# Eight more gather buffers and eight more sample buffers in the first four stages of a deformable-convolution and mixture-of-experts kernel

## The chip, the cores and the metric

The kernel runs on one core of one Trainium2 chip. The metric is device time in microseconds: 7486.86 us is the median of three runs before the change. Engines are named as in the profile: PE is TensorE (PEld its weight loads), ACT is ScalarE, DVE is VectorE, POOL is GpSimd, SP is SyncE. They run at once and wait for each other through semaphores; each works through its own instructions in order.

## The reference, cut to what matters

An image batch of 4 x 256 channels x 64 x 64 goes through three deformable 3x3 convolutions and then, as tokens, through a mixture of eight experts with the two best of each token.

```python
x0 = ln_c(x)                                   # normalised over channels
for w_off, b_off, w, b in three_layers:
    om   = conv3x3(x0, w_off) + b_off          # 27 channels: 9 x (dy, dx), 9 masks
    ys, xs = grid + taps + om[:, :18]          # 9 sampling points of each pixel
    smp  = bilinear(x0, ys, xs) * sigmoid(om[:, 18:])    # [B, 256, 9, H, W]
    x0   = relu(einsum("bikhw,oik->bohw", smp, w) + b)
x = x + x0
t = tokens(x)                                  # 16384 x 256
p = softmax(ln(t) @ gate_w + gate_b); keep the best two of eight
t = t + sum over the two of p_e * (gelu(ln(t) @ W1_e + b1_e) @ W2_e + b2_e)
```

## The kernel before, in words

The convolutions run as twelve stages, one for each layer `l` and image `b`, in the order that `run` lists: (0,0), (1,0), (0,1), (2,0), (1,1), (0,2), (2,1), (1,2), (0,3), (2,2), (1,3), (2,3). Stage 3, layer 2 of image 0, is thus the one that finishes the first image. A stage has eight blocks `n` of 512 pixels; a block has nine taps `k`; a tap has four tiles of 128 pixels. So a stage is 72 taps and 288 samples.

For each sample, `samples` does four things. POOL issues an indirect DMA that gathers, for 128 pixels, a row of 1024 numbers (the four neighbours of the sampling point, L503) from a table in DRAM into a tile `g`. VectorE blends the neighbours in two instructions (L509 in place in `g`, L514 from `g` into a tile `s`). ScalarE scales `s` by mask and corner weight, in place (L517). The tiles `g` come from a ring of `GB = 10` buffers (`gat`), the tiles `s` from a ring of 8 (`smp`). A gather waits until VectorE has read the buffer's last tenant, and L514 waits until TensorE has read the last tenant of its `s`.

`turn` lags two pairs of samples behind (`LAG`): TensorE transposes a pair (L532) into PSUM and ScalarE copies it into `sT` (L535). When both pairs of a tap are there, `finish` multiplies the tap before it with its weights into `acc` (L555). After the ninth tap ScalarE takes `acc` to the next layer's window (L577), or, in layer 2, to `tokens`. In a stage's last block `finish` also loads the next stage's weights tap by tap on SP (`wk`, L477).

Side work is spread between the taps by `step` and `pump`, as generators that go on by a piece. `off_block` makes the plan of a later block: the offset convolution (L357), `om` (L366), `pm` (L371), `pos` (L391, on VectorE from L395) and so on to indices and weights. `pre_block` normalises an image that comes later: a load `xc`, transposes (L442), `h_pre` (L447, normalised at L62 to L78), stores into its table (L338) and transposes into the window (L462). In stages 0, 3 and 6 the next images' `pre_block`s run beside. `tokens`, beside stages of layer 2 and the head of the stage after them, loads the input again (`xr_tok`, L596), adds (L599), transposes (`t_tok`, L613), computes logits and normalises (`st_tok` L62, `lg_tok`, `sm_tok` L665) and stores (L626, L636). Where a generator must not go ahead of the samples, its instructions are placed on the engine after the newest sample, with `with self.after(self.last)`.

The experts start once an image's tokens are routed, from stage 4 on. They use three pools: `ffn` (their activations, and `ta`, the token rows that the results are added to, L902), `rt` (routing) and `gyp` (gathered results).

All pools are opened at the start and stay open to the end. A scheduler in the language layer places the instructions on each engine's queue from the program's order and the tiles' dependences, and puts in the semaphore waits. Indirect DMAs on POOL carry eight semaphores in turn, and a gather also waits for the one eight before it.

Of the kernel before, what the change touches and what calls it, by code (L numbers as in the profile page):

```python
# [8 lines left out]
F32 = mybir.dt.float32  # L9
# [5 lines left out]
P = 128  # L15
H = W = 64
C = 256
CC = C // P
K = 9
NL = 3  # L20
# [15 lines left out]
FT = 1 << FT_LOG  # L36
FU = FT // P
GB = 10
LAG = 2
LEAST = 2.0**-30  # L40
WINN = CC * (RPB + 2) * W
# [41 lines left out]
class Group:  # L83


    def __init__(self, b, n0, n1):
        self.b, self.n0, self.n1 = b, n0, n1
        self.nm = f"{b}_{n0}"
        self.M = (n1 - n0) * TPB

        self.NF = 2 * self.M * P // FT + E - 1


        self.half = (self.NF + 1) // 2
        self.zt, self.acc, self.gy, self.sums, self.py = {}, [], [], [], None
        self.order = [s // 2 + s % 2 * self.half for s in range(self.NF)]
# [21 lines left out]
class Weave:  # L118
# [3 lines left out]
    def __init__(self, ctx, tc, ins, out):  # L122
        nc = self.nc = tc.nc
        self.tc = tc
        self.ins = ins
        self.x = ins["x"].rearrange("b (c p) h w -> b p c (h w)", p=P)
        self.out_v = out.rearrange("b (c p) h w -> b p c (h w)", p=P)
        self.B = self.x.shape[0]

        def pool(name, bufs, **kw):  # L130
            return ctx.enter_context(tc.tile_pool(name=name, bufs=bufs, **kw))

        self.cst = pool("cst", 1)
        self.dram = pool("dram", 1, space=bass.MemoryType.DRAM)
        self.wkp = pool("wkp", 1)
        self.plan = pool("plan", 19)
        self.win = pool("win", 3)
        self.wt = pool("wt", 2)
        self.small = pool("small", 1)
        self.big = pool("big", 2)  # L140
        self.ffn = pool("ffn", 2)
        self.rt = pool("rt", 1)
        self.rt2 = pool("rt2", 2)
        self.gyp = pool("gyp", 4)
        self.smT = pool("smT", 2)
        self.smp = pool("smp", 8)
        self.gat = pool("gat", GB)
        self.ps = pool("ps", 3, space=bass.MemoryType.PSUM)
        self.ps1 = pool("ps1", 1, space=bass.MemoryType.PSUM)

        self.routes, self.tiles, self.sums = Lane(), Lane(), Lane()
        self.side, self.plans_side = [], []
        self.last = self.gathered = self.turned = None
        self.starting, self.draining, self.later = True, False, []
        self.pend, self.pairs = None, []
# [319 lines left out]
    def load_tap(self, l, k, i):  # L475
# [3 lines left out]
        )  # L479
        self.wk[k] = wk  # L480

    def main_block(self, i, n, wins):
        l, b = self.stages[i]
        plan = self.plans.pop((l, b, n))
        for k in range(K):
            for t0 in range(0, TPB, 2):
                ss = self.samples(i, n, k, t0, plan)
                self.pairs.append((i, n, k, t0, wins, ss))
                if len(self.pairs) > LAG:
                    self.turn()  # L490
            self.step(k)
            self.pump()

    def samples(self, i, n, k, t0, plan):


        nc = self.nc
        idx, cf = plan
        ss = []
        for t in (t0, t0 + 1):  # L500
            j = t * K + k
            g = self.gat.tile([P, 2, 2, C], F32, tag="g", name=f"g_{i}_{n}_{j}")
            self.gathered = nc.gpsimd.indirect_dma_start(  # L503
                out=g.rearrange("p x s f -> p (x s f)"),
                out_offset=None,
                in_=self.table(*self.stages[i]),
                in_offset=bass.IndirectOffsetOnAxis(ap=idx[:, j : j + 1], axis=0),
            )
            nc.vector.scalar_tensor_tensor(  # L509
                g[:, :, 0, :], g[:, :, 1, :], cf[:, j, 0:1], g[:, :, 0, :],  # L510
                ALU.mult, ALU.add,
            )
            s = self.smp.tile([P, C], F32, tag="s", name=f"s_{i}_{n}_{j}")
            self.last = nc.vector.scalar_tensor_tensor(  # L514
                s, g[:, 1, 0, :], cf[:, j, 1:2], g[:, 0, 0, :], ALU.mult, ALU.add
            )
            nc.scalar.activation(s, s, AF.Copy, scale=cf[:, j, 2:3])  # L517
            ss.append(s)
        return ss
# [515 lines left out]
    def run(self):  # L1035

        self.stages = [
            (0, 0), (1, 0), (0, 1), (2, 0), (1, 1), (0, 2),
            (2, 1), (1, 2), (0, 3), (2, 2), (1, 3), (2, 3),
        ]  # L1040

        beside = {0: 1, 3: 2, 6: 3}


        last = self.B - 1
        self.groups = [Group(b, 0, NB) for b in range(last)]
        self.groups += [Group(last, 0, NB // 2), Group(last, NB // 2, NB)]

        for i, (g, pace) in enumerate(zip(self.groups, (5.0, 5.0, 2.0, 1.5, 0.0))):
            g.i, g.pace, g.last = i, pace, i + 1 == len(self.groups)  # L1050
        self.plans = {}
        wins = {}
        pre = [self.pre_block(0, n, wins, n // 2 % 2 == 0) for n in range(NB)]
        for gen in pre[:3]:
            next(gen)
        self.constants()
        self.tables_init()
        for n, gen in enumerate(pre):
            for _ in gen:
                pass  # L1060

            for later in pre[n + 1 : n + 2]:
                for _ in range(3):
                    next(later)
            for later in pre[n + 3 : n + 4]:
                next(later)
            self.settle()
        self.starting = False
        for k in range(K):
            self.load_tap(0, k, 0)  # L1070
        self.ffn_constants()
        for i, (l, b) in enumerate(self.stages):
            wins, pre = {}, {}
            for n in range(NB):
                for gen in self.later[:2]:
                    self.aside(6, gen, True)
                self.later = self.later[2:]
                self.main_block(i, n, wins)
                if i in beside:
                    self.aside(5, self.pre_block(beside[i], n, pre, i == 0))  # L1080
            if i + 1 == len(self.stages) or self.stages[i + 1] == (l + 1, b):
                while self.pairs:
                    self.turn()
                self.finish()
                self.settle()
        while self.routes.pieces or self.tiles.pieces or self.sums.pieces:
            self.drain(3)
# [48 lines left out]
```

## Time and profile before

| | |
|---|---|
| median of three runs | 7486.86 us (7480.8 to 7520.67) |
| the profiled execution | 7520.62 us, its span 7518.9 us |
| busy, share of the span | PE 86%, PEld 48%, DVE 66%, ACT 43%, POOL 60% |
| granted TensorE clock | 0.944 |
| DMA engines | 2223.73 MB, mean 296 GB/s; 73.3% of their time in POOL's indirect DMAs |
| gathers | 3456 of 128 rows of 4 KB each |

Windows that fall on the gathers of the first stages (us from the start of the span): stage 0 93 to 652, stage 1 652 to 1118, stage 2 1118 to 1597, stage 3 1597 to 2095. A window's row gives the busy time of each engine, with the number of instructions in brackets. In a row of waits, "A <- B: total, times, longest" means that engine and line A sat idle until B ended; "issue" is idle time for which no releaser is seen, and "remote" a releaser that the profile doesn't name. The groups of instructions give count, busy time, mean duration and, after the second bar, idle time before them with what ended it.

### The profile page before, as it was taken

To read this page: it belongs to the slowest core of one execution; us is meant where nothing else is said; L and a number is where in the kernel's file an instruction comes from. 1 tells how busy PE (TensorE), PEld (TensorE's weight loads), DVE (VectorE), ACT (ScalarE), POOL (GpSimd) and SP (SyncE) were. 2 spreads that over 40 slices of the span, in tenths; PEclk is the share of its full clock that TensorE was granted. 3 is DMA by queue.
4 is the path that set the end of the run, shared out by engine and by line. 5 is a ranking of instruction groups with operands and counts; after the bars stand their busy time and mean duration, and the time that the engine had idled before them with its cause. 6 is when DMAs were issued, how large, how long until landed. Compare 5 with 4: busy or idle time off the path is not lost.

```text
span 7518.9 us, 88985 instructions
## 1 busy us (share of the span) xinstructions
PE 6443.2 (86%) x26500; PEld 3618.8 (48%) x26500; DVE 4952.9 (66%) x11467; ACT 3266.0 (43%) x7141; POOL 4476.5 (60%) x4245
## 2 busy tenths in 40 slices
PE   6898888888898888889988888888888788977887
PEld 3443333334454444445554445444544555644565
DVE  6776777768887666567777556666768554667421
ACT  3444544445544444445443434444444333444322
POOL 4654666656666565556557656555656565666543
PEclk8999999999999999999999999999999899989998
DMA  8997999989998888888888888888888777888644
GB/s 266 337 325 274 352 342 335 346 331 356 362 349 311 300 305 297 278 315 322 314 293 316 293 280 314 295 302 294 308 306 299 251 271 240 288 302 287 211 139 123
DMA packets 800320, 2223.73 MB, mean 296 GB/s; under 512 B 104729, under 2 KB 302873, under 8 KB 794081
## 3 DMA queue, kind: packets, MB, share of 16 engines
q0 software_dynamic: 551200, 1947.35, 73.3%
q1 hardware_dynamic: 248640, 270.69, 10.9%
q8 instruction: 215, 3.52, 0.2%
q14 instruction: 265, 2.16, 0.1%
HBM read 2160.68 MB, written 196.40 MB: 313 GB/s over the span
## 4 chain that ended last, share of the span: by engine, by line
PE 69%; ACT 10%; issue 7%; another core or an unknown queue 6%; DVE 4%; DMA 2%; POOL 1%; SPq 0%; ACTq 0%; DVEq 0%; POOLq 0%
PE acc L555 34%; PE tp L532 10%; PE ph L856 7%; PE py L874 6%; PE po L357 6%; ACT sT L535 4%; ACT s L517 3%; DVE g L509 2%; DVE s L514 1%; PE pm L371 1%; ACT hT L866 1%; PE ftp L840 1%; ACT win L577 1%; PE tpv L325 1%
## 5 line engine op out<-in xcount | busy, mean ns | idle before, releaser
L503 POOL DMA_INDIRECT g<-tab,idx x3456 | 3685.4, 1066 | 2371.6 <-DVE s L514 1061.8
L555 PE MATMUL acc<-sT,wk 128*128 128x512 f32 x6912 | 3492.1, 620 | 253.4 <-ACT sT L535 147.5
L509 DVE SCALAR_TENSOR_TENSOR g<-g,cf 128x512 f32<-128x512 f32 x3456 | 2559.2, 742 | 269.1 <-DMA g<-tab,idx 245.5
L514 DVE SCALAR_TENSOR_TENSOR s<-g,cf 128x256 f32<-128x256 f32 x3456 | 1662.7, 483 | 1331.3 <-PE tp L532 729.9
L535 ACT COPY sT<-tp 128x512 f32<-128x512 f32 x1728 | 1002.0, 585 | 2312.0 <-PE tp L532 1553.0
L517 ACT ACTIVATE s<-s,cf 128x256 f32<-128x256 f32 x3456 | 1629.5, 508 | 256.7 <-DVE s L514 160.7
L555 PEld LDWEIGHTS acc<-sT,wk 128*128 128x128 f32 x6912 | 1198.9, 198 | 1106.7 <-issue 816.7
L532 PEld LDWEIGHTS tp<-ident,s 128*128 128x128 f32 x6912 | 893.2, 146 | 1666.2 <-issue 898.9
L532 PE MATMUL tp<-ident,s 128*128 128x128 f32 x6912 | 1287.3, 286 | 439.2 <-ACT s L517 253.8
L856 PE MATMUL ph<-fzT,w 128*128 128x256 f32 x2608 | 720.8, 411 | 78.0 <-ACT fzT L844 28.1
L874 PE MATMUL py<-w,hT 128*128 128x256 f32 x2608 | 671.1, 396 | 103.5 <-ACT hT L866 58.0
L856 PEld LDWEIGHTS ph<-fzT,w 128*128 128x128 f32 x2608 | 506.3, 205 | 212.9 <-issue 69.6
L874 PEld LDWEIGHTS py<-w,hT 128*128 128x128 f32 x2608 | 484.5, 196 | 242.0 <-issue 91.9
L866 ACT ACTIVATE hT<-ph,w 128x256 f32<-128x256 f32 x652 | 281.9, 471 | 616.3 <-PE ph L856 378.2
L812 POOL DMA_INDIRECT zt<-z,tok x326 | 333.8, 1024 | 161.5 <-issue 88.0
L800 POOL DMA_INDIRECT w<-in_W,wrow x163 | 178.0, 1092 | 381.2 <-issue 138.8
L357 PE MATMUL po<-win,wo 128*32 128x504 f32 (+1 forms) x2304 | 366.0, 615 | 6.5 <-ACT win L301 4.2
L892 DVE TENSOR_TENSOR y<-py,w 128x512 f32<-128x512 f32 x163 | 111.9, 686 | 341.5 <-PE py L874 285.1
L915 POOL DMA_INDIRECT gy<-ys,slots x256 | 255.6, 998 | 104.5 <-issue 70.0
L930 DVE SCALAR_TENSOR_TENSOR ta<-gy,cw,ta 128x256 f32<-128x256 f32 x256 | 120.6, 480 | 125.6 <-DMA gy<-ys,slots 78.4
L357 PE MATMUL po<-win_pre,wo 128*32 128x504 f32 (+1 forms) x1152 | 184.2, 617 | 2.0 <-ACT om L366 2.0
L366 ACT ACTIVATE om<-po,bo 128x512 f32<-128x512 f32 x96 | 65.9, 687 | 265.3 <-PE po L357 156.3
(154 smaller groups left out, 2961.0 us busy)
## 6 DMA issues: line engine op xcount, KB each, us to landing
tab<-hv SPq DMA_DIRECT2D x512, 128.0 KB
g<-tab,idx POOLq DMA_INDIRECT x3456
ys<-y SPq DMA_DIRECT2D x163, 256.0 KB
tab<-h_pre SPq DMA_DIRECT2D x128, 256.0 KB
wk<-in_conv_w SPq DMA_DIRECT2D x99, 256.0 KB
xc_pre<-in_x SPq DMA_DIRECT2D x32, 512.0 KB
xr_tok<-in_x SPq DMA_DIRECT2D x32, 512.0 KB
t<-t_tok SPq DMA_DIRECT2D x32, 512.0 KB
```

The lines of the kernel that those rows point to most:

```text
L357: nc.tensor.matmul(po[g * Q : (g + 1) * Q, :].rearrange("q (r w) -> q r w", w=W)[:, :, x0:x1], lhsT=self.wo[l][:, 3 * ky + kx, c, :], rhs= ...
L503: self.gathered = nc.gpsimd.indirect_dma_start(out=g.rearrange("p x s f -> p (x s f)"), out_offset=None, in_=self.table(*self.stages[i]), ...
L509: nc.vector.scalar_tensor_tensor(g[:, :, 0, :], g[:, :, 1, :], cf[:, j, 0:1], g[:, :, 0, :], ALU.mult, ALU.add,)
L514: self.last = nc.vector.scalar_tensor_tensor(s, g[:, 1, 0, :], cf[:, j, 1:2], g[:, 0, 0, :], ALU.mult, ALU.add)
L517: nc.scalar.activation(s, s, AF.Copy, scale=cf[:, j, 2:3])
L532: self.turned = nc.tensor.transpose(tp[:, c, u * P : (u + 1) * P], ss[u][:, c * P : (c + 1) * P], self.ident)
L535: nc.scalar.copy(self.sT[:, :, t0 * P : (t0 + 2) * P], tp)
L555: nc.tensor.matmul(acc[:, o, :], lhsT=self.wk[k][:, c, o * P : (o + 1) * P], rhs=sT[:, c, :], start=(k == 0 and c == 0), stop=(k == K - 1 ...
L812: self.nc.gpsimd.indirect_dma_start(out=zt, out_offset=None, in_=grp.zd, in_offset=bass.IndirectOffsetOnAxis(ap=grp.tok[:, j : j + 1], axi ...
L856: nc.tensor.matmul(ph[:, h, :], lhsT=w1[:, o : o + P], rhs=zT[:, c, :], start=(c == 0), stop=(c == CC - 1),)
L866: nc.scalar.activation(ht[:, h, :], ph[:, h, :], AF.Gelu, bias=w1[:, k : k + 1])
L874: nc.tensor.matmul(py[:, u, :], lhsT=hT[h // 2][:, h % 2, u * P : (u + 1) * P], rhs=w2[:, h * C : (h + 1) * C], start=(h == 0), stop=(h == ...
```

## The change

The pools `ffn`, `rt` and `gyp` are no longer opened at the start. Two pools of eight buffers, `gatx` and `smpx`, are opened in an `ExitStack` of their own, `early`. A counter `drawn` takes the tile `g` from `gat` ten times and from `gatx` eight times in turn, and `s` from `smp` eight times and from `smpx` eight times: rings of 18 and 16. When the stage after (2, 0) begins, which is stage 4, `late_pools` closes `early`, sets the rings back to `gat` (10) and `smp` (8), and opens `ffn`, `rt` and `gyp` on the room that came free. The tiles of the last samples of stage 3 that TensorE has yet to transpose are kept by the dependences that the language layer records.

```diff
+GS = 8
+GX = 8
@@ __init__
-        self.ffn = pool("ffn", 2)
-        self.rt = pool("rt", 1)
         self.rt2 = pool("rt2", 2)
-        self.gyp = pool("gyp", 4)
         self.smT = pool("smT", 2)
-        self.smp = pool("smp", 8)
+        self.smp = pool("smp", GS)
         self.gat = pool("gat", GB)
+        self.pool = pool
+        self.early = ctx.enter_context(ExitStack())
+        more = [
+            self.early.enter_context(tc.tile_pool(name=name, bufs=GX))
+            for name in ("gatx", "smpx")
+        ]
+        self.gats = [self.gat] * GB + [more[0]] * GX
+        self.smps = [self.smp] * GS + [more[1]] * GX
+        self.drawn = 0
@@
+    def late_pools(self):
+
+        self.early.close()
+        self.gats, self.smps = [self.gat], [self.smp]
+        self.ffn = self.pool("ffn", 2)
+        self.rt = self.pool("rt", 1)
+        self.gyp = self.pool("gyp", 4)
@@ samples
-            g = self.gat.tile([P, 2, 2, C], F32, tag="g", name=f"g_{i}_{n}_{j}")
+            g = self.gats[self.drawn % len(self.gats)].tile(
+                [P, 2, 2, C], F32, tag="g", name=f"g_{i}_{n}_{j}"
+            )
@@
-            s = self.smp.tile([P, C], F32, tag="s", name=f"s_{i}_{n}_{j}")
+            s = self.smps[self.drawn % len(self.smps)].tile(
+                [P, C], F32, tag="s", name=f"s_{i}_{n}_{j}"
+            )
+            self.drawn += 1
@@ run
             wins, pre = {}, {}
+            if self.stages[i - 1] == (NL - 1, 0):
+                self.late_pools()
             for n in range(NB):
```

## The prediction

> **What bounds the kernel now.** The page comes first. Its costliest idle time, read by size, makes the change look large.
>
> ```profile
> L503 POOL DMA_INDIRECT g<-tab,idx x3456 | 3685.4, 1066 | 2371.6 <-DVE s L514 1061.8
> L514 DVE SCALAR_TENSOR_TENSOR s<-g,cf 128x256 f32<-128x256 f32 x3456 | 1662.7, 483 | 1331.3 <-PE tp L532 729.9
> ```
>
> POOL sits idle before gathers until VectorE has written a sample (a gather buffer comes free), and VectorE sits idle before samples until TensorE has transposed one (a sample buffer comes free). Both are waits for buffers, and the change doubles these buffers in stages 0 to 3. But a wait for a buffer is back pressure: it says that the waiting engine is ahead. What counts is what the engine behind all of them, TensorE, waits for. The windows of the four stages concerned, second column on: length, then busy time of PE, PEld, DVE, ACT, POOL, then clock, DMA share, GB/s:
>
> ```profile
> 93.00:652.00 559.00, 488.29 (x2064) 221.20 (x2058) 406.38 (x1015) 254.21 (x575) 310.22 (x289) 0.96 0.88 312
> 652.00:1118.00 466.00, 387.99 (x1465) 175.49 (x1466) 340.40 (x675) 214.90 (x475) 306.10 (x288) 0.96 0.93 340
> 1118.00:1597.00 479.00, 411.64 (x1564) 186.62 (x1563) 347.47 (x689) 226.38 (x501) 307.18 (x288) 0.97 0.92 339
> 1597.00:2095.00 498.00, 435.22 (x1791) 225.31 (x1792) 421.44 (x1101) 250.60 (x548) 315.71 (x288) 0.95 0.96 356
> ```
>
> TensorE is busy 83 to 87% in each. In stages 1 and 2 VectorE is busy 73%; in stage 3, which adds the image-2 normalisation and the token work, 85%. The chain of waits in the middle of stage 1 (start, length, what) shows one whole tap:
>
> ```profile
> 1000.10 0.85 PE tp L532 x4
> 1000.97 0.59 ACT sT L535
> 1001.61 1.12 PE acc L555 x2
> 1002.74 0.22 PE tp L532 x2
> 1002.95 1.72 PE acc L555 x4
> 1004.67 0.23 PE tp L532 x2
> 1004.98 0.58 ACT sT L535
> 1005.57 0.42 ACT s L517
> 1006.03 0.85 PE tp L532 x4
> ```
>
> A tap takes 1006.03 - 1000.10 = 5.93 us, and the chain passes through TensorE and ScalarE alone: no DVE, POOL or DMA. The transposes at 1006.03 wait for a scaling `s`, and that scaling waits for nothing but its place on ScalarE behind the copy of the transposes before. 72 taps of 5.93 are 427 us; eight offset convolutions of 4.9 us (the chain's `po` pieces) add 39; together 466, the length of stage 1. So the loop explains the stage. The view of line 517 in stages 1 and 2 (652 to 1597) says the same: what ScalarE waited for before scaling, and who waited for it.
>
> ```profile
> its engine sat idle before it (us, times) until:
>   DVE s L514: 7.3, 6
> who waited for it (us, times):
>   PEld tp L532: 152.8, 231
> ```
>
> In 945 us ScalarE waits 7.3 us for samples to scale. I also counted, over the trace's rows, how far each engine is ahead whenever TensorE starts the transposes of a tap. In stages 1 and 2 it is nearly always gathers issued 16 to 18, samples written 8, samples scaled 1 to 3. All buffers are full; ScalarE's order limits the scaling. A sample lies some 9.6 us between VectorE and ScalarE, and a gather, from its packets, lands about 5.1 us after its issue and then lies 8 us unread (medians).
>
> **The change, part by part.** The order of instructions on PE, DVE, ACT and POOL is the same in both programs; no operation is added or removed. What changes are waits. The program does what its description says: gathers 11 to 18 lose their wait on VectorE, and a sample waits for the transposes of sixteen samples before in place of eight.
>
> Stages 1 and 2, and the steady part of stage 0: the gather lead grows from 18 towards 34 and the sample lead from 8 towards 16. VectorE needs 4 x (0.742 + 0.483) = 4.9 us of a 5.93 us tap and fills this. TensorE's loop does not contain it, so the gain is 0. What hides it is that same loop; if ScalarE were ahead, the gain would at most be the 7.3 us above.
>
> At this place a page speaks for the change: "Perfetto Trace Analysis", section Identifying Performance Opportunities, says that the same gap repeating on the engine that should be saturated can mean too few buffers for the next tile. TensorE does have such a gap, 0.68 us before `acc` and 0.28 before `tp` in each tap, and if both came from buffers the change would return 0.96 x 72 x 3, some 200 us. The rows name ScalarE's copy and scaling as their releasers, with samples lying ready, so the sum goes by the rows.
>
> Stage 3 and the head of stage 0 are where samples are late at times. The waits of ScalarE over all four stages (93 to 2095), then TensorE's in stage 3 (1597 to 2095):
>
> ```profile
> ACT s L517 <- DVE s L514: 45.8, 40, 10.4
> ACT s L517 <- DVE sq_pre L74: 8.3, 7, 1.2
> ACT s L517 <- DVE sq_pre L73: 4.9, 6, 0.8
> ```
> ```profile
> PE tp_pre L462 <- DVE h_pre L78: 20.8, 7, 4.8
> PE tp L532 <- ACT s L517: 5.6, 10, 1.6
> ```
>
> With 4.7 us more before `DVE g`, ScalarE waits 64 us for VectorE in the four stages, 11.9 of it in stage 0 (10.4 is the very first sample, which no buffer brings sooner). But TensorE in stage 3 loses only 5.6 us before transposes that follow such a scaling, and 20.8 us before the normalised rows `h_pre`: 26 us is the most stage 3 can return directly. What the buffers can supply is VectorE's idle time before samples in that stage: 9.3 us until TensorE, 13.3 with an unnamed releaser, 8.2 "issue", so 31 us. Most of it is one stall of 1.6 to 3.7 us in each block, at the first sample of tap 6 (line 514), and that stall goes.
>
> What is late next is written in VectorE's order. Between the samples stand instructions of the side work that wait for ScalarE: in each block of stage 3 `st_tok` may run only when VectorE is at most 2 or 3 samples ahead of ScalarE's scaling, `sm_tok` 3, `st_pre` 3 or 4. These places are 8 to 16 samples apart, so a lead of 16 is cut down four times in 36 samples. In stages 1 and 2 only `pos` does so, at 11, once a block, and the window's memset at 3, once a stage. The lead that stage 3 inherits (8 samples x 1.23 = 10 us) is cut by `pos` at its twelfth sample. In three blocks VectorE already waits at `st_pre` (9.2 us until `h_pre` L447), so part of any time won there is handed to that wait.
>
> So the gain in stage 3 lies between 0 (every stall removed returns at the next of these places) and 26 us, and I take 8: one stall of about 2.5 us in each of eight blocks is 20 us, of which the places downstream let less than half through. For stage 0, without the first sample, 1.5 us before `s` and one wait of 2.3 us until `DVE g` remain, and I take 2 of these 4.
>
> The late pools: from stage 4 on the ring is the old one, 10 and 8 buffers. Before the first tile of `ffn`, `rt` and `gyp` stands a wait for the last use of `gatx` and `smpx`. The routing's first matmul comes after the last transposes of stage 3 in any case, and the gathers it waits for have long landed: 0. On SP three loads `ta` of image 0 move from early in stage 3 to between the loads `wk` of taps 6, 7 and 8, where the first waits for the last sample of stage 3, ended at 2109.4. Queued behind it on SP are `wk` 7 and 8, the last `xr_tok`, four table stores and the next `xc_pre`. `wk` 7 waits for TensorE's use of tap 7, and that stage's last `acc` ends at 2118, so the added delay is 0 to 5 us, and `wk` 7 is not needed for some 40 us more: 0. In exchange SP no longer stands behind the store of the first two token blocks: some us, off the path. The first and last users of both early pools lie in order, so no barrier is added.
>
> Sum: 0 (stages 1, 2) - 8 (stage 3) - 2 (stage 0) + 0 (pools, SP) = -10 us. The profiled execution took 7520.6 us (span 7518.9) and would take about 7511; the runs' median is 7486.86, with 7480.8 to 7520.67 as spread, and the same 10 us makes 7477.
>
> **Rivals.** *Faster*: stalls behind late samples go altogether, because a lead once built survives the side work. For it: ScalarE's 64 us. Against it: the caps in VectorE's order. Its price is 26 us in stage 3 for TensorE's direct waits, up to 64 if each late scaling is on the path: 7423 to 7461, in the middle 7442; from 7449 down it is past half a per cent.
>
> *Slower*: gathers that run further ahead crowd SP's transfers in stage 3. The DMA share there is already 0.96 at 356 GB/s. Eight semaphores serve the gathers, so eight can be in flight, where now some 5.3 / 1.48 = 3.6 are; a load of `xr_tok` or `xc_pre` behind them would land up to 4.4 x 1.48 = 6.5 us later. If VectorE stands before it each time, eight blocks lose 52 us: 7539. Against it: in the steady state each gather still waits for a freed buffer, so the rate stays, and eight are in flight only for a moment. It decides from about 4.7 us per block.
>
> *Nothing*: every stall comes back downstream, 7487; this lies within the forecast's class.
>
> **How the numbers follow.** Half a per cent, 37 us, is about what a measurement of this kernel can tell from no change. Forecast (0 to 26 us gained): 0.85. Past half a per cent faster: 0.10. Slower by that much: 0.05. The range reaches down to 7442, the middle of the faster case, and up to 7521, the highest run of before, since the median of few runs can land there.
>
> **What would show it.** Right: in stages 1 and 2 the tap stays at 5.93 us with the same chain, DVE's waits before `s` move to `pos`, POOL's waits before `g` stay; stage 3 is some 8 us shorter; stage 4 on is unchanged. Wrong: a tap under 5.8 us in stage 1, stage 3 shorter by over 30 us, or new waits for `xr_tok` and `xc_pre`.

## The result, and the profile after

The change made the kernel slower: 7739.32 us (median of 4 runs, 7734.06 to 7742.18) beside 7492.04 us of the kernel before (7480.8 to 7520.67), a ratio of 1.0314, 95% interval 1.0288 to 1.034. The profiled execution took 7734.06 us, its span 7732.3 us, with a mean granted clock of 0.933. The forecast was 7477 us and "no change".

First, where the time went. The windows of stages 0 to 3 in the profile after (columns as before: length, busy time of PE, PEld, DVE, ACT, POOL, clock, DMA share, GB/s):

```profile
94.00:728.00 634.00, 497.95 (x2080) 225.28 (x2072) 405.75 (x1015) 254.03 (x574) 300.56 (x288) 0.91 0.77 275
728.00:1237.00 509.00, 394.39 (x1440) 178.00 (x1438) 329.51 (x648) 211.07 (x466) 299.43 (x288) 0.91 0.85 307
1237.00:1769.00 532.00, 425.09 (x1563) 193.63 (x1562) 348.70 (x691) 226.00 (x499) 300.00 (x289) 0.93 0.84 305
1769.00:2294.00 525.00, 441.86 (x1762) 223.05 (x1763) 420.90 (x1102) 248.22 (x546) 310.36 (x288) 0.93 0.90 336
```

VectorE, ScalarE and GpSimd are busy for about as long as before, but the clock, 0.95 to 0.97 before, is 0.91 to 0.93, and the DMA engines carry less per second. Something stands still. From the first to the last transpose of a stage (L532 before, L553 after), stage 0 took 604.3 us (528.5 before), stage 1 536.3 (473.0), stage 2 531.7 (475.6), stage 3 508.6 (491.3): 212 us in all. From stage 4 on the difference stays about the same: each later stage begins 212 to 224 us later than before, and the spans differ by 213.

The forecast's tap is still there. The longest pieces of the chain of waits in stage 1 after (start, length, what):

```profile
1002.06 0.85 PE tp L553 x4
1002.93 0.59 ACT sT L556
1003.57 1.12 PE acc L576 x2
1004.91 1.72 PE acc L576 x4
1006.94 0.59 ACT sT L556
1007.99 0.85 PE tp L553 x4
```

1007.99 - 1002.06 = 5.93 us, through TensorE and ScalarE, as before. The loss lies between such taps. Some forty microseconds later the chain shows

```profile
1043.38 0.59 ACT sT L556
1043.96 1.20 ACT s L538 x3
1045.16 6.75 another core or an unknown queue
...
1051.99 0.59 ACT sT L556
```

"Another core or an unknown queue" is what the view says when an engine goes on at a semaphore event that matches no end of an instruction. The timeline of that moment tells which. Rows are start, duration, engine, line, operation, with the idle time before in square brackets:

```profile
1044.98 0.38 PE L553 MATMUL tp<-ident,s 128*128 128x128 f32 x2
1045.19 1.88 PE L576 MATMUL acc<-sT,wk 128*128 128x512 f32 x4
1046.91 0.38 PE L553 MATMUL tp<-ident,s 128*128 128x128 f32 x2
1047.13 1.02 PE L576 MATMUL acc<-sT,wk 128*128 128x512 f32 x2
1047.99 0.38 PE L553 MATMUL tp<-ident,s 128*128 128x128 f32 x2
...
1051.99 0.59 ACT L556 COPY sT<-tp 128x512 f32<-128x512 f32 x1 [6.83 <-remote]
...
1048.11 0.75 DVE L527 SCALAR_TENSOR_TENSOR g<-g,cf 128x512 f32<-128x512 f32 x1
1051.92 0.48 DVE L535 SCALAR_TENSOR_TENSOR s<-g,cf 128x256 f32<-128x256 f32 x1 [3.07 <-remote]
...
1046.14 0.97 POOL L521 DMA_INDIRECT g<-tab,idx  x1 [0.30 <-issue]
1047.41 0.98 POOL L521 DMA_INDIRECT g<-tab,idx  x1 [0.30 <-issue]
1048.70 0.97 POOL L521 DMA_INDIRECT g<-tab,idx  x1 [0.30 <-issue]
1052.67 1.21 POOL L521 DMA_INDIRECT g<-tab,idx  x1 [3.01 <-DVE s L535]
```

TensorE's last transposes end at 1048.37. ScalarE's copy of them and VectorE's next sample both wait for TensorE and start together, at 1051.99 and 1051.92. In the trace's record of the semaphore that TensorE counts up, one step stands at 1043.35 and the next three at 1051.84, 1051.92 and 1051.97. In that time TensorE ran three pairs of transposes, which end at 1045.36, 1047.29 and 1048.37, with four products `acc` and then two between them. The profile models these ends; but had TensorE itself stood still, its three steps would lie some 3.0 us apart, as that work does. They lie within 0.13 us, so the work was done and its signals were held: the last came 3.6 us late, the first 6.5. Meanwhile GpSimd had been issuing gathers back to back, one each 1.28 us (0.97 + 0.30), until the sample ring was full.

The Trainium skill, "Perfetto Trace Analysis", section Tensor Engine Instruction, says that TensorE's end in a profile is modelled, and that the semaphore is pushed only when PSUM has acknowledged the last bytes, then spreads. This trace agrees that the two moments differ, here by 3.6 us.

I call a copy `sT` late when it starts over 1 us after its transposes ended with ScalarE idle. In stages 0 to 3 of before there are 18, together 47.9 us; after, 50, together 225.3 us. The difference, 177 us, is most of the 212. The rest may come with the clock: in these stages it stood at half for 166 us before and 362 us after. The two can't be added, since half-clock time may fall into a wait. Not every signal is late: where ScalarE waited for a sample of VectorE in these stages after the change, it began within 0.04 us of the sample's end each time. The view of ScalarE's waits over these stages (after 100 to 2328, then before 99 to 2113) shows most of the late copies as its "remote" row:

```profile
ACT sT L556 <- PE tp L553: 637.5, 354, 6.5
ACT sT L556 <- remote: 202.8, 34, 23.2
```
```profile
ACT sT L535 <- PE tp L532: 619.3, 385, 5.7
ACT sT L535 <- remote: 53.7, 12, 10.6
```

### The profile page after: what moved, and what is told of

Same layout as the page of the kernel before. It is cut to its first block, busy times and chain, and to the rows that moved or that the text cites. A ratio compares the mean times of both kernels' runs of the same rounds, so it can differ in the third digit from the quotient of the medians.

```text
span 7732.3 us, 88839 instructions
## 1 busy us (share of the span) xinstructions
PE 6491.1 (84%) x26500; PEld 3639.1 (47%) x26500; DVE 4950.0 (64%) x11467; ACT 3265.8 (42%) x7141; POOL 4447.1 (58%) x4245
## 4 chain that ended last, share of the span: by engine, by line
PE 66%; ACT 9%; issue 9%; another core or an unknown queue 8%; DVE 4%; DMA 2%; POOL 2%; SPq 0%; ACTq 0%; POOLq 0%; DVEq 0%
PE acc L576 33%; PE tp L553 10%; PE ph L877 7%; PE py L895 6%; PE po L365 6%; ACT sT L556 3%; ACT s L538 3%; DVE g L527 1%; DVE s L535 1%; PE pm L379 1%; DMA g<-tab,idx 1%; POOL g L521 1%; ACT hT L887 1%; PE ftp L861 1%
## 5 line engine op out<-in xcount | busy, mean ns | idle before, releaser
L576 PE MATMUL acc<-sT,wk 128*128 128x512 f32 x6912 | 3539.0, 627 | 369.1 <-ACT sT L556 154.2
L553 PEld LDWEIGHTS tp<-ident,s 128*128 128x128 f32 x6912 | 898.0, 147 | 1724.2 <-issue 957.5
L553 PE MATMUL tp<-ident,s 128*128 128x128 f32 x6912 | 1291.7, 288 | 485.9 <-ACT s L538 261.3
L403 DVE TENSOR_TENSOR pos<-pos,base 128x72 f32<-128x72 f32 x96 | 22.0, 229 | 273.8 <-ACT pos L399 272.8
```

The costliest lines, as they stand in the source:

```text
L553: self.turned = nc.tensor.transpose(tp[:, c, u * P : (u + 1) * P], ss[u][:, c * P : (c + 1) * P], self.ident)
L576: nc.tensor.matmul(acc[:, o, :], lhsT=self.wk[k][:, c, o * P : (o + 1) * P], rhs=sT[:, c, :], start=(k == 0 and c == 0), stop=(k == K - 1 ...
```

## The experiments

Theories at the start. *Saturation*: longer rings let gathers run free for longer, the DMA engines fill up, and TensorE's signals come late until all rings are full. *Placement or order*: the new pools' place or the late pools' order costs the time. *Which ring* was open too.

The experiments ran in six groups (e, f, g, h, k, m), each beside the kernel before on the same device, and the devices differ. With e, g and k the kernel before took 6804 to 6808 us and no copy was late in any profile, in any stage: I call these quiet devices. With f, h and m it took 7620, 7506 and 7627 us, with late copies as in the profiles above: late devices. These are three devices, so late copies of one group are compared with those of another across devices.

**Each part by itself, quiet device.** The first keeps the pools by phase, with rings of 10 and 8; the next two lengthen one ring each; the fourth is the whole change, with gathers spaced.

```diff
 # e1_layout
-        self.gats = [self.gat] * GB + [more[0]] * GX
+        self.gats = [self.gat]
-        self.smps = [self.smp] * GS + [more[1]] * GX
+        self.smps = [self.smp]
 # e2_gather18: only the line of self.smps;  e3_sample16: only that of self.gats
 # e4_after_pace: after each gather of stages 0 to 3
+                    self.gathered = nc.gpsimd.memset(self.pace, 0.0)   # 128 x 128
```

> The changed kernel with its pools opened by phase, but with the rings kept at 10 gather and 8 sample buffers (the sixteen extra buffers are reserved and not used). Saturation theory (longer rings let gathers run free for longer, the transfers saturate, and TensorE's completion signals come late): the old time, 7470 to 7515 us. Placement theory (moved pools, other addresses or the late pools' waits cost it): the new time, 7700 to 7760 us.

> Only the gather ring is 18, the sample ring stays 8. Saturation theory: bursts are longer only where VectorE has stood still and the gather ring has filled, so a part of the loss, 7500 to 7620 us. Order theory (VectorE with more samples in hand runs into the side work's waits, and these cost the time): no loss, 7470 to 7515 us, since VectorE's lead over TensorE is still 8.

> Only the sample ring is 16, the gather ring stays 10. Saturation theory: VectorE runs free twice as long, at 1.28 us a sample against some 1.46 us that a gather's transfer needs, so most of the loss, 7600 to 7740 us; with ten gather buffers fewer gathers can be in flight, so not all of it. Order theory: all of the loss, 7700 to 7760 us.

> The changed kernel with a memset of 128x128 on POOL after each gather of stages 0 to 3 (some 0.2 us by the memset of the identity in the trace), so that gathers are issued no faster than about one in 1.5 us instead of 1.28. Saturation theory: the late signals go, stages 0 to 3 shrink by 150 to 230 us, 7480 to 7590 us. Order theory and placement theory: no change or slower, 7720 to 7800 us, since VectorE's order, its waits and the pools are the same.

The expectations were worked out for the device of the result; on this one only the ratios can be held against them, and since no signal is late on it, the runs don't decide between the theories. Measured, beside 6803.81 us: e1 6803.45 us, ratio 1.0003 (0.9993 to 1.0012); e2 6807.9 us, 1.0003 (0.9993 to 1.0012); e3 6801.99 us, 0.9996 (0.9987 to 1.0006); e4 6883.76 us, 1.0117 (1.0101 to 1.0134). So on this device pools by phase cost nothing, neither ring gains or costs anything where signals are on time, and spacing the gathers (1.33 us at least, less than the 1.5 that I expected) costs time there. Stage 3 took 460 us in e1, 458 in e2 and 453 in e3.

**The same on a late device.** The change itself, each ring alone, and four more buffers of each kind (`GX = 4`).

> The changed kernel as it is, beside the kernel before on the same chip. Two theories. T1 (the device sets the price): the 18 gather and 16 sample buffers only cost time where TensorE's signals come late; then on a chip whose kernel before takes about 6804 us and shows no copy of sT that starts over 1 us after its four transposes, the change gives 6800 to 6812 us (nothing), and on one whose kernel before takes about 7490 us with some 48 us of late copies in the first four stages it gives 7700 to 7760 us. T2 (the change sets the price): the two longer rings together make the loss whatever the chip, which neither ring alone did in e2_gather18 and e3_sample16; then 6980 to 7040 us beside 6804.

> Only the gather ring is longer (18), the sample ring stays at 8. Beside a kernel before of about 6804 us: nothing, as in e2_gather18. Beside one of about 7490 us: if it is the number of gathers that POOL may issue ahead that makes TensorE's signals late, as with both rings, 7680 to 7760 us; if it is the samples that VectorE runs ahead with, 7480 to 7520 us.

> Only the sample ring is longer (16), the gather ring stays at 10. Beside a kernel before of about 6804 us: nothing. Beside one of about 7490 us: if the gathers in flight decide, the ring of 10 still holds POOL back and the time is 7480 to 7560 us; if the samples decide, 7680 to 7760 us.

> The change with four more buffers of each kind in place of eight (14 and 12). Beside a kernel before of about 6804 us: nothing. Beside one of about 7490 us: half of the loss, 7580 to 7640 us, if the loss grows with the length of the rings; all of it, 7700 to 7760 us, if it comes with the order of the pools or as soon as POOL is free to run past ten gathers.

Measured, beside 7619.59 us: f1 7849.71 us, 1.0304 (1.027 to 1.0338); f2 7631.71 us, 1.0016 (0.9994 to 1.0039); f3 7865.14 us, 1.0317 (1.0273 to 1.0361); f4 7739.23 us, 1.0152 (1.0112 to 1.0193). The result repeats, the sample ring makes all of it, the gather ring nothing, and four more buffers make half. ScalarE's "remote" waits, of f2 (98 to 2140) and of f3 (97 to 2359), tell the same:

```profile
ACT sT L556 <- remote: 54.7, 10, 10.7
```
```profile
ACT sT L556 <- remote: 245.0, 39, 12.9
```

This went against my first guess that gathers in flight decide: with f3 the gather ring still holds GpSimd to ten.

**Place, and a shorter ring, quiet device.** One has all eight sample buffers in the new place; one takes six in place of eight in the kernel before.

```diff
 # g1_far8 (the kernel after)
+        self.gats = [self.gat]
+        self.smps = [more[1]]
 # g2_sample6 (the kernel before)
+        self.smp = pool("smp", 6)
```

> The kernel after with a gather ring of 10 and a sample ring of eight, as long as before, but all eight sample buffers of the first four stages are the new ones, where the experts' buffers lie later. If the place of the new buffers in memory costs the time, half of the buffers at that place cost 3.2 % (f3_sample16), so all of them cost 3 to 6 %: 7840 to 8070 us beside a kernel before of 7620 us. If the length of the ring costs it, nothing: ratio 0.997 to 1.003. On a chip where the kernel before takes about 6804 us both give nothing and the run tells nothing apart.

> The kernel before with six sample buffers in place of eight, in all twelve stages. If every sample by which VectorE may run ahead lengthens the stretches in which TensorE's signals are late (3.2 % for eight more buffers, 1.5 % for four), two fewer give ratio 0.985 to 0.997 beside a kernel before of 7620 us, and the copies of sT that start over 1 us late in the first four stages sum to less than 48 us. If eight is already so short that TensorE runs dry when VectorE turns to other work, two fewer cost more than they give: ratio 1.003 to 1.02, and so it is on a chip where the kernel before takes 6804 us.

Beside 6805.76 us: g1 6807.62 us, 1.0 (0.999 to 1.0009), which tells nothing apart here; g2 6836.27 us, 1.0048 (1.0031 to 1.0065), so eight is already short enough to cost if cut.

**Half the bytes, quiet device.** The gather brings the first of its two rows alone.

```diff
-                out=g.rearrange("p x s f -> p (x s f)"),
+                out=g[:, 0, :, :].rearrange("p s f -> p (s f)"),
```

> The kernel after, but each gather brings only the first of its two rows (half of the bytes, as many descriptors and instructions), and VectorE takes the second row's values from the first: the second row's part of the samples is left out. Theory of the full queues: TensorE's signals come late while the gathers keep all DMA engines busy (P of a late signal 0.02 with up to four gathers in flight, 0.62 with seven); with half the bytes the engines are busy half the time, no copy of sT starts over 1 us late in the first four stages (sum under 20 us, now 225 us), and the time is that of g4_half_before within 0.3 %. Theory of the run-ahead alone: VectorE and GpSimd running free hold TensorE's signals up whatever the bytes; then the late copies stay at 150 to 230 us and the ratio to g4_half_before is 1.02 to 1.035.

> The kernel before with the same half-size gathers, as the base of g3_half_after. Theory of the full queues: late copies of sT in the first four stages under 10 us; beside a kernel before of 7620 us it takes 6850 to 7300 us, since the later stages lose their late signals too; beside one of 6804 us, 6760 to 6805 us. Theory of the run-ahead alone: late copies stay at some 48 us and the time within 1 % of the kernel before.

g3 took 7603.81 us, 1.1171 (1.1152 to 1.119), and g4 7614.29 us, 1.1188 (1.1169 to 1.1207); no late copy in either. Both expectations for g4 missed: with half the bytes the kernel was 12% slower. VectorE waited for landings, which it hardly did with whole gathers. The waits of g4 (95 to 2090) and of g1 in the same stretch:

```profile
DVE g L509 <- DMA g<-tab,idx: 498.0, 516, 9.5
```
```profile
DVE g L527 <- DMA g<-tab,idx: 14.7, 13, 10.6
```

A half gather shows as some 64 packets of 4096 bytes, of 220 ns in the mean, where a whole one has some 128 of 172 ns: so its cost is not half. But the 12% can't be put down to the bytes. The edit also changed the order in which the scheduler placed the instructions: before, 10% of the transposes of stage 1 run in rows of eight or more, between which TensorE does the products, and in g3 and g4 88%. Half a gather lands sooner, 3.3 us after its issue in the median of stages 1 and 2, where g1 has 5.5; but VectorE blends with only 3 gathers issued ahead, its own among them, where g1 has 9. Why so few, no run shows. As a base for the next group the pair serves: long rings against short make no difference in it.

**Place, rate and bytes, late device.** g1 and g3 again, and the sample ring of 16 with gathers spaced.

```diff
 # h2_paced16 (sample ring 16, gather ring 10), stages 0 to 3
+                    self.gathered = nc.gpsimd.memset(self.pace, 0.0)   # 128 x 240
```

> The kernel of g1_far8 again: a gather ring of 10, a sample ring of eight that lies wholly in the new place. g1_far8 ran where no signal of TensorE was late, so the place is still open. Beside a kernel before of about 7500 to 7620 us: if the place of the buffers costs the time, ratio 1.03 to 1.06 and late copies of sT in the first four stages of 200 us or more; if the length of the ring, ratio 0.997 to 1.004 and late copies of 40 to 80 us. Beside a kernel before of about 6805 us: nothing by both.

> Gather ring 10, sample ring 16 as in f3_sample16, and in the first four stages GpSimd clears a scratch tile of 128 x 240 after each gather (218 ns for 128 columns in e4_after_pace, which raised the least spacing of gathers from 1.25 to 1.33 us), so that gathers come no faster than 1.43 to 1.48 us, the spacing that they have while all rings are full. Beside a kernel before of 7500 to 7620 us, full queues: the late copies of sT fall from 224 us to under 80 us, and the time is 0.995 to 1.02 of before, since catching up is slower too. The length of the ring in itself, whatever the rate: late copies stay over 180 us and the ratio is 1.04 to 1.06. Beside a kernel before of 6805 us: ratio 1.012 to 1.03 by both.

> The kernel of g3_half_after again (both rings long, half of each gather's bytes, the second row's part of the samples left out), to be held against its own 7603.81 us where no signal was late. Beside a kernel before of 7500 to 7620 us, full queues: late copies of sT in the first four stages under 20 us and a time within 0.5 % of 7604 us, with the DMA engines at 0.6 of their time. Run-ahead whatever the bytes: late copies over 100 us and 7750 to 7900 us. Beside a kernel before of 6805 us it repeats 7604 us and tells nothing.

Beside 7505.65 us: h1 7511.5 us, 1.0 (0.9983 to 1.0018); h2 7508.62 us, 1.0009 (0.9986 to 1.0032); h3 7858.58 us, one run. The place is out: h1 has 57.2 us of late copies, about as many as before. Spacing takes the loss away: the least gather spacing in h2 is 1.42 us and one copy is late in stages 0 to 3, 5.3 us, where f3, on another late device, has 223.9. That the device of h2 is a late one, its own later stages show, which have no spacing: 109 late copies, 360 us. h1, on the same device, shows the rate by itself. For each copy of its stages 0 to 3 I took the last six gathers issued before its transposes ended, if the sixth came at most 2.5 us before that end. Where these six started within 6.5 us, 16 of 31 copies were late; where they took over 7.0 us, 1 of 421. In h2 no six start within 7.0 us. On the quiet device of e3 six gathers stood within 6.5 us before 227 copies, and none was late. ScalarE's "remote" row of h2 (98 to 2101):

```profile
ACT sT L560 <- remote: 5.3, 1, 5.3
```

And *saturation* falls: h3 has 200.2 us of late copies (55, in the profile of its one run), and its first four stages take 2121 us where g3 took 2014, with the DMA engines busy 0.58 to 0.61 of the time. The windows of its stages 0 to 2:

```profile
98.00:630.00 532.00, 437.33 (x1892) 221.15 (x1893) 378.28 (x962) 247.84 (x556) 333.64 (x285) 0.89 0.61 179
671.00:1200.00 529.00, 404.55 (x1457) 198.41 (x1457) 349.12 (x690) 223.21 (x497) 374.65 (x306) 0.86 0.58 169
1204.00:1703.00 499.00, 402.68 (x1560) 197.66 (x1559) 338.46 (x685) 221.84 (x498) 294.86 (x286) 0.90 0.60 172
```

So the bytes don't decide. What was left: the spacing of h2 slows VectorE with GpSimd. Which of them holds the signals up?

**Half as many gathers.** Sample ring 16, and in stages 0 to 3 one gather serves two samples; VectorE, ScalarE and TensorE keep all their instructions, though in another order: in rows of eight or more run 89% of the transposes of stage 1, much as in h3. A second run spaces the gathers of the kernel before in all twelve stages, to see whether that gives a faster kernel.

```diff
 # k1_one_for_two, m1_one_for_two
+            if i >= 4 or t == t0:
+                g = self.gats[self.drawn % len(self.gats)].tile(
...
+                self.gathered = nc.gpsimd.indirect_dma_start(
...
 # k2_pace_all (the kernel before), all stages
+                    self.gathered = nc.gpsimd.memset(self.pace, 0.0)   # 128 x 240
```

> Gather ring 10, sample ring 16 as in f3_sample16, but in the first four stages only every other gather is made, and VectorE takes the second sample of each pair from the same gathered rows (half of the gathered data is left out); VectorE, ScalarE and TensorE have as many instructions as before, and VectorE can sample every 1.23 us (0.745 + 0.484), as fast as ever. Beside a kernel before of 7500 to 7620 us: if it is the rate of the gathers that makes TensorE's signals late, no copy of sT in the first four stages starts over 1 us late (sum under 15 us, 224 us in f3_sample16) and these stages take 430 to 470 us each; if it is VectorE running ahead, the late copies stay over 150 us and the stages take 500 us or more. Beside a kernel before of 6805 us both give stages of 400 to 450 us and the run tells nothing apart.

> The kernel before (rings of 10 and 8) with the scratch clear of 128 x 240 after each gather in all twelve stages. Rate of the gathers: beside a kernel before of 7500 to 7620 us the late copies of sT fall from some 370 us over all stages to under 60 us, and the time to 7050 to 7400 us, less than both kernels. Length of the rings alone: no fewer late copies, 7500 to 7700 us. Beside a kernel before of 6805 us it only slows the catching up: ratio 1.015 to 1.04.

> The kernel of k1_one_for_two again (sample ring 16, one gather for two samples in the first four stages, half of the gathered data left out), which ran where no signal was late and took 6835 us. Beside a kernel before of 7500 to 7620 us: if the rate of the gathers makes TensorE's signals late, the late copies of sT in the first four stages sum to under 15 us; if VectorE's running ahead does, to over 150 us. Beside one of 6805 us it repeats 6835 us.

k1 and k2 fell on a quiet device: 6835.02 us, 1.0043 (1.0026 to 1.006), and 7234.36 us, 1.0632 (1.0615 to 1.065), beside 6807.63 us. The cost of k2 is more than the 1.04 that I allowed (its order, too, is not quite that of before), and stages 0 and 3 of k1 are longer than the 400 to 450 us that I gave for such a device. m1 ran on a late one: 7514.71 us beside 7627.2 us, 0.9853 (0.9831 to 0.9875), with 14.0 us of late copies. Its stages 0 to 3 took 460.2, 435.5, 446.9 and 495.8 us there and 460.6, 434.9, 450.5 and 492.7 us in k1: where the gathers are halved, the late device is as fast as the quiet one. From stage 4 on, where m1 gathers for each sample again, it has 115 late copies, 374 us. Leaving half of the data out also moves the sampling points of the layers that follow; stages 0 and 2, of the first layer, keep theirs, and have two late copies, 3.4 us, between them. The windows of m1's first two stages show VectorE busier than the kernel before in these stages (0.82 and 0.79 of the time; 0.73 there), and GpSimd at about half:

```profile
99.00:559.00 460.00, 416.58 (x1891) 214.04 (x1892) 377.22 (x962) 248.23 (x557) 203.13 (x140) 0.95 0.63 206
600.00:1035.00 435.00, 374.15 (x1449) 186.69 (x1450) 344.62 (x684) 226.80 (x497) 235.35 (x153) 0.94 0.63 206
```

VectorE runs ahead in m1 as well: when TensorE starts the transposes of a tap, 11 to 16 samples are written ahead of it at 221 of the 288 taps (before, never over 8). ScalarE keeps close behind VectorE, as its waits show (99 to 1985):

```profile
ACT s L539 <- DVE s L536: 617.0, 453, 8.8
ACT sT L557 <- remote: 6.8, 4, 2.7
```

The nearest run to hold m1 against is h3: half of the bytes too, an order of the same kind, 11 to 16 samples ahead at 225 taps, a late device. It has twice as many gathers, and 200.2 us of late copies where m1 has 14.0. So on these devices it is GpSimd's gathers, close behind each other, that make TensorE's signals late; neither their bytes nor VectorE's lead does. In h2, too, VectorE has a long ring to fill, and the signals are on time.

**How the sample ring comes in.** I counted in the traces, over stages 0 to 3, gathers that are the seventh or later of a row without a pause (spacing up to 1.36 us), and the share of them issued during a late copy:

| kernel | gathers, samples in ring | late copies, us | seventh or later in a row | of these late | other gathers late |
|---|---|---|---|---|---|
| before | 10, 8 | 47.9 | 48 | 0.25 | 0.01 |
| h1 | 10, 8 | 57.2 | 52 | 0.15 | 0.02 |
| f2 | 18, 8 | 68.3 | 72 | 0.26 | 0.01 |
| f4 | 14, 12 | 150.5 | 70 | 0.30 | 0.05 |
| f3 | 10, 16 | 223.9 | 156 | 0.55 | 0.05 |
| after | 18, 16 | 225.3 | 189 | 0.42 | 0.07 |
| e3, quiet | 10, 16 | 0 | 455 | 0 | 0 |
| e2, quiet | 18, 8 | 0 | 115 | 0 | 0 |

With all rings full, gathers come at the pace of TensorE's taps, 5.93 / 4 = 1.48 us. Only while the sample ring is filling up do they run at 1.28 us, and a longer sample ring takes longer to fill: on quiet devices it makes four times as many gathers in long rows. On late devices a late signal itself stops TensorE, which lets the row go on until the ring is full, so a longer ring also allows a longer stall. A longer gather ring changes little, because VectorE, stopped by its sample ring, is what stops GpSimd in the end. The counts and the runs show that the ring lengthens the rows and that the signals are late in them; that each stall feeds itself in this way is argued from the timeline above, not tested. h3 doesn't fit the count of rows: it has only 27 such gathers and yet 200 us. Its gathers land in another way, but its lateness goes with their rate too: with six gathers issued in the 8 us before the transposes ended, 43 of 155 copies were late, with up to four none of 292.

What stays open: why one device's signals come late and another's don't; what path the gathers and TensorE's signals share, if they share one; whether the signals are late without the profiler, since each run on record has a profiled span; and the full change on a quiet device, where only its parts ran. k2 was not run on a late device: if the late signals of all stages went there, its 7234 us would be less than before's 7492, by estimate 3%, at a cost of 6% on a quiet one. No version tried that keeps all the data beats both kernels.

## Why the prediction was wrong

**The step that failed** is the 0 for stages 1 and 2 and the steady part of stage 0: "TensorE's loop does not contain it, so the gain is 0. What hides it is that same loop". The loop was read rightly (5.93 us before, and after in the taps that nothing disturbs), and the lead does grow (to 16 samples written and 33 or 34 gathers issued at more than half of the taps of stages 1 and 2) without return. But the loop's link from TensorE to ScalarE is a signal, and on late devices that signal comes late when gathers are issued close behind each other. The term had no price for a loss; it measured +76, +63 and +56 us in stages 0 to 2, where the forecast had -2, 0 and 0. The profile before held the clue, unpriced: "another core or an unknown queue 6%" in the chain of a kernel on one core, and the 53.7 us of ScalarE's waits for `sT` with a "remote" releaser shown above, beside the 45.8 us for VectorE that the forecast did use.

**The rival slower** had the right sign and half of a mechanism: gathers running ahead in bursts cost something else its time. It had the wrong victim (loads on SP in stage 3), the wrong ring and too low a price, 52 us. It was set aside with "the rate stays, and eight are in flight only for a moment". The rate does not stay while the ring is filling, and a longer sample ring makes that moment longer. Stage 3, its place, lost least: 17 us.

**A misreading beside the point.** For VectorE's idle time before samples in stage 3 the prediction adds 8.2 us of "issue"; the view of 1597 to 2095 has 3.0, so the sum is 26 us and not 31, and the stall at tap 6 stands in six of the eight blocks and not in each. The forecast of 8 us doesn't move by it.

**Right, as far as the runs go.** The late pools and the moved loads cost nothing that was measured: e1 1.0003 on a quiet device, h1, with the same pools, 1.0 on a late one, and the stages from 4 on lose nothing more. VectorE's waits moved to `pos` in part: those before `s` until TensorE's transposes went from 135.8 us (652 to 1597 before) to 102.1 (728 to 1769 after), those at `pos` from 20.4 to 135.1. The rows before and after:

```profile
DVE pos L395 <- ACT pos L391: 20.4, 3, 11.0
```
```profile
DVE pos L403 <- ACT pos L399: 135.1, 14, 20.5
```

How much of the 135 us is a late signal that reached VectorE by way of ScalarE, I did not separate. On the quiet device the long sample ring made stage 3 shorter by 7 us (460 to 453, one profile each; 8 was forecast) and the whole by nothing that could be measured. The page's reading of repeating gaps as too few buffers, which would have returned some 200 us, was rightly set behind the rows: with signals on time neither ring returned anything.

## What to carry to other kernels

A buffer that removes back pressure can still cost: it lets the engine ahead run at its own full rate for longer, and that rate may disturb something else. Before lengthening a ring, ask at what rate the producer runs while it fills, and look for waits of the bottleneck whose releaser the profile can't name; where an engine goes on long after its releaser's last end, look at the semaphore's own record. Try such a change on more than one device, since the same two kernels were 3% apart on one and their parts alike on another.

## What the runs showed of the hardware

The devices differ by about a tenth on the same program: 6804 to 6808 us on some, 7492 to 7627 us on others, with equal durations of single instructions (the median `acc` matmul 592 ns and the first VectorE blend 745 ns in f2, 592 and 744 in e2). On the latter TensorE's completion signals come up to 19.7 us late (f1), several within some 0.1 us of each other (three within 0.13 us above), while TensorE, VectorE and GpSimd work on until they too wait; on the former, no copy `sT` started over 1 us late. A gather of half the bytes landed 3.3 us after its issue, a whole one 5.5 (g3, g1, medians of stages 1 and 2); yet the programs with half gathers were 12% slower on a quiet device, in an order that differs too. Clearing 128 x 240 numbers on GpSimd after each gather, which put the least spacing at 1.42 us in place of 1.25, was enough to bring the signals back in time on a late device (h2, one late copy in four stages).
